# Transposing normalised rows through DRAM blocks and VectorE in place of TensorE and ScalarE

## The chip, the cores and the metric

The kernel runs on one core of a Trainium2 chip. The metric is the device time of one execution in microseconds, as the median of three runs. The engines are named as in the profile: PE is TensorE's matmuls, PEld its weight loads, DVE is VectorE, ACT is ScalarE, POOL is GpSimd, and SP is SyncE, whose only work here is to issue all DMAs, in one queue, in program order.

## What is computed

Two layers on a batch of 16 graphs of 1024 nodes with 256 channels, all in float32.

```python
# layer 0: aggregate over the normalised adjacency, two-layer perceptron with batch norms
x = _layernorm(x + _L0_gnn_ref(x, adj, W1, ..., be2))
# layer 1
c_adj = mean of x over channels                       # (B, N)
A     = |  |sigmoid(c_adj_j - c_adj_i) - 0.5| - 0.5 | * 2     # made symmetric
g     = relu(einsum('bcn,bnm->bcm', x^T, adj * A) * para)      # queries, channels first
k, v  = split(x @ kv_w)                                # 4 heads of 64
out   = softmax(q k^T * scale) v
x     = _layernorm(x + out)
```

The change concerns the x that enters layer 1, called x1 below. It is needed twice: with nodes on partitions (for the graph product and the last residual), and with channels on partitions, as x1T, because keys and values contract over channels.

## The kernel before

**Two stages.** Stage one, until about 820 us, is layer 0 up to the second batch norm's moments; its result y lies in DRAM. Stage two, `fast()`, takes the batches one by one: it finishes layer 0 for a batch, prepares layer 1 and runs attention. A general path, lines 1084 to 1193, is there for unusual softmax denominators and isn't entered.

**Steps and slots.** Attention of one batch is 16 steps (`step`, line 727). A step is `scores` (16 matmuls of 64x64 on 512 columns, line 739), `exps` (two exponentials on ScalarE, line 751), `sums` (VectorE adds them up for the denominators, lines 757 and 760) and `attend` (16 matmuls, line 770). All other work is cut into pieces and put into slots by `put(w, t, ...)`: batch w has slots 0 to 7. The loop from line 1055 emits the pieces of two slots, then four steps: slots 0 and 1, four steps, slots 2 and 3, four steps, and so on. This emission order is the order of each engine's queue; nothing reorders it later.

**The pieces that matter here.** In the slots of batch b-2 (lines 896 to 905), for each pair j = 0..3 of row blocks of batch b (one pair is 256 nodes):
- `load(b, j)`, slot j: four DMAs of 64 KB bring y in 32x32 blocks (`y_blk`, line 432), one DMA brings the old x (line 436)
- `bn2_q`, slot j+1: GpSimd applies batch norm 2 (line 599)
- `rows`, slot j+2: VectorE transposes the blocks (line 603), so that nodes lie on partitions, and adds x (line 604)
- `ln1_a`, slot j+2, and `ln1_b`, slot j+3: layer norm on VectorE (lines 547, 548, 624), with 1/sqrt on GpSimd (lines 66, 68); line 624 also gives the row sums
- `x1_t`, slot j+4: four TensorE transposes of 128x128 into PSUM (line 638) and a copy into x1T (line 639), by ScalarE for all batches but the first
- `means`, slot 6, and `crow`, slot 7: the row means (lines 642 and 644) are transposed (line 659), copied (line 661), and written to DRAM and read back on all partitions (lines 662 and 663)

In the slots of batch b-1: `wg_a` and `wg_b` (gates, slots 0 to 3, lines 671 to 680), `keys` (slots 0 and 1, line 688), `values` (slots 1 and 2, line 699), `graph` (32 products of 128x512, six or seven in each of slots 3 to 7, line 713) with `queries` after each eighth one (lines 721 and 722). In a batch's own slots, `dens`, `recips`, `finish_a`, `finish_s` and `finish_b` end each half of its nodes; `finish_b` issues the store of the result (line 841).

For batch 1 the slots of batch b-2 are slots -8 to -1. They are emitted before any attention, interleaved with the graph product of batch 0 (`opening`, line 1044), whose `queries` come in slot -1, and followed by `scores(0)`. Batch 0 itself has code of its own (lines 1018 to 1042) and keeps its TensorE transposes.

**Order inside a slot.** `arrange` (line 944) spreads pieces that are "short" on TensorE among the long ones and puts all others behind the last piece of lower or equal rank in `order` (line 930). `behind` (line 1058) marks the last short piece; `sums` of the next step is emitted there.

**Buffers.** The tag `yt` has two buffers (LDP = 2), x1T one per batch in flight (a pool of one), PSUM tag `t` four, exponentials six.

Of the kernel before, what the change touches and what calls it, by code (L numbers as in the profile page):

```python
# [9 lines left out]
F32 = mybir.dt.float32  # L10
# [6 lines left out]
P = 128  # L17
# [5 lines left out]
def gnn_norm_attention_kernel(  # L23
# [16 lines left out]
    nc = tc.nc  # L40
    B, N, C = x.shape
    H = W1.shape[0]
    NT = N // P
    CT = C // P
    HT = H // P
    FB = 512
    NH = N // FB
# [4 lines left out]
    dram = ctx.enter_context(tc.tile_pool(name="dram", bufs=1, space=DRAM))  # L52
# [28 lines left out]
    Q = 32  # L81
    NQ = P // Q
    y_blk = [yT_all[b].rearrange("i (d e) (q n) -> q e (i d) n", e=Q, q=NQ) for b in range(B)]
    st2_dram = dram.tile([2, C], F32, name="st2_d")

    c_dram = [dram.tile([NT, P], F32, name=f"crow_d{b}") for b in range(B)]
# [33 lines left out]
    with ExitStack() as l0:  # L120
# [32 lines left out]
        with ExitStack() as ph1:  # L153
# [9 lines left out]
            for i in range(0, NT, 2):  # L163
                t = hp.tile([P, 2, N], F32, tag="h", name=f"A{i}")
# [29 lines left out]
            for h in range(NH):  # L194
                rows = range(h * KB, (h + 1) * KB)
                for i in rows:
                    blk = A[i][:, ts(i, P)]
# [8 lines left out]
                for j in range(NT):  # L206
                    p = ps.tile([P, FB], F32, tag="ah"[j % 2], name="pat")
# [25 lines left out]
            for c in range(HT):  # L233
                p = ps.tile([P, FB], F32, tag="a", name="pw1")
# [3 lines left out]
            for c in range(CT):  # L238
                p = ps.tile([P, FB], F32, tag="a", name="pw2")
# [120 lines left out]
            def hidden(b, h, f):  # L360
                p = ps.tile([P, FB], F32, tag="h", name="ph")
                for k in range(CT):
                    nc.tensor.matmul(
                        p,
                        W1T[:, k, ts(f, P)],
                        aggT[b][:, k, ts(h, FB)],
                        start=(k == 0),
                        stop=(k == CT - 1),
                    )
                return p  # L370
# [11 lines left out]
            for f in range(HT):  # L382
                for h in range(NH):
# [3 lines left out]
                    p = hidden(B - 1, h, f)  # L387
# [7 lines left out]
        ldp = right("ldp", LDP)  # L395
# [43 lines left out]
        with ExitStack() as ph2:  # L439
# [74 lines left out]
            for k, pair in enumerate(pairs):  # L514
# [4 lines left out]
                if not ahead:  # L519
                    for j in range(LDP):  # L520
                        load(0, j)
                    for j in range(LDP, NT // 2):
                        t = accp.tile([P, 2, FB], F32, tag="acc", name=f"first{j}")
# [32 lines left out]
    def fast():  # L556
      with ExitStack() as fx:
# [15 lines left out]
        x1s, x1Ts, css, crows, mvs, wgs = {}, {}, {}, {}, {}, {}  # L573
# [46 lines left out]
        def ln1_b(b, j):  # L620
            mv, rs = mvs.pop((b, j))
            for a in range(2):
# [8 lines left out]
                    accum_out=css[b][:, 2 * j + a : 2 * j + a + 1],  # L631
                )

        def x1_t(b, j):
            p = ps_t.tile([P, CT, 2 * P], F32, tag="t", name="px")
            for a in range(2):
                for c in range(CT):
                    nc.tensor.transpose(p[:, c, ts(a, P)], x1s[b, j][:, a, ts(c, P)], ident)  # L638
            (nc.vector.tensor_copy if b == 0 else nc.scalar.copy)(x1Ts[b][:, :, ts(j, 2 * P)], p)  # L639

        def means(b):
            nc.vector.tensor_scalar_mul(css[b], css[b], 1.0 / C)
# [233 lines left out]
        def put(w, t, f, *a):  # L876
            at.setdefault(w * NC + t, []).append((f, a))
# [4 lines left out]
        for b in range(B):  # L882

            for hf in range(NH):
                t = (hf + 1) * (NC // NH)
                put(b, t, dens, b, hf)
                put(b, t + 1, recips, b, hf)
                for k in range(KB // 2):
                    put(b, t + 1 + k, finish_a, b, hf * (KB // 2) + k)
                    put(b, t + 1 + k, finish_s, b, hf * (KB // 2) + k)  # L890
                    late = NC - t - 2 - k if b == B - 1 and hf == 0 else 0
                    put(b, t + 2 + k + late, finish_b, b, hf * (KB // 2) + k)
            if b == 0:
                continue

            put(b - 2, 2, begin, b)
            for j in range(NT // 2):
                put(b - 2, j, load, b, j)
                put(b - 2, j + 1, bn2_q, b, j)
                put(b - 2, j + 2, rows, b, j)  # L900
                put(b - 2, j + 2, ln1_a, b, j)
                put(b - 2, j + 3, ln1_b, b, j)
                put(b - 2, j + 4, x1_t, b, j)
            put(b - 2, NC - 2, means, b)
            put(b - 2, NC - 1, crow, b)

            i = 0
            for t, n in enumerate(WG):
                for i in range(i, i + n):
                    put(b - 1, t, wg_a, b, i)  # L910
                    put(b - 1, t, wg_b, b, i)
                i += 1
            kv = [(keys, (b, c, h)) for c in range(CT) for h in range(NH)]
            kv += [(values, (b, j)) for j in range(0, NT, 2)]
            for t, n in enumerate(KV):
                for _ in range(n):
                    f, a = kv.pop(0)
                    put(b - 1, t, f, *a)
            m = 0
            for t, n in enumerate(QG):  # L920
                for m in range(m, m + n):
                    put(b - 1, NC - len(QG) + t, graph, b, m)
                m += 1
# [3 lines left out]
        nsteps = B * NS  # L927


        order = (dens, recips, finish_a, finish_b, x1_t, rows, ln1_a, ln1_b, finish_s, means, load, crow)  # L930
        rank = {f: k for k, f in enumerate(order)}
        short = (dens, recips, finish_a, x1_t, crow)
        long = (keys, values, graph)

        def spread(few, many):
# [119 lines left out]
        for t in range(min(at) // 2, max(max(at) // 2, nsteps // NK - 1) + 1):  # L1055
# [3 lines left out]
            for k in range(len(now) + 1):  # L1059
                if k == behind and 0 <= g < nsteps:  # L1060
                    sums(g)
                if k < len(now):
                    f, a = now[k]
# [15 lines left out]
        )  # L1079

    flag = fast()


# [153 lines left out]
```

## Time and profile before

| | before |
|---|---|
| time, median of 3 (range) | 2548.84 us (2546.09 to 2551.68) |
| span of the profiled execution | 2546.3 us |
| mean granted TensorE clock | 0.993 |
| PE, DVE, ACT, POOL busy | 98%, 68%, 42%, 34% |
| DMA: bytes, packets, of these under 512 B | 163.79 MB, 233,349, 136,680 |

Times in the profile are microseconds from the span's start. In a group of instructions the columns are line, engine and operation, tile written and tiles read with their shapes, count, then total busy time and the mean of one in nanoseconds, then the idle time of the engine just ahead of them and what ended it. In a timeline the columns are start, duration, engine, line, operation, tiles, count of merged neighbours, and in brackets the idle time before with its releaser. A matmul's duration is not its price where matmuls overlap; there the distance from one start to the next is the better measure. A long float32 product is issued as several instructions, so counts in the profile are multiples of the source's.

### The profile page before, as it was taken

How to read it: one execution, taken by the hardware profiler on the slowest of the kernel's cores; microseconds unless marked ns; L12 is line 12 of the kernel's file. 1: busy time of each engine (PE TensorE's matmuls, PEld its weight loads, DVE VectorE, ACT ScalarE, POOL GpSimd, SP SyncE). 2: the span in 40 equal slices, each digit the busy share in tenths (PEclk: the TensorE clock that was granted, in tenths of full speed). 3: DMA queues.
4: the chain of work that ended last, by engine and by line, in shares of the span. 5: the costliest groups of instructions: out<-in, count | busy, mean ns of one | idle time of the engine just before them, and what ended most of it. 6: DMA issues, size and time to landing. Idle time of an engine off the chain costs nothing. (4 is left out here: it accounts for less than half of the span.)

```text
span 2546.3 us, 33280 instructions
## 1 busy us (share of the span) xinstructions
PE 2487.9 (98%) x12813; PEld 1067.4 (42%) x12813; DVE 1730.6 (68%) x2594; ACT 1078.3 (42%) x1385; POOL 865.3 (34%) x766
## 2 busy tenths in 40 slices
PE   8999999998998999999999999999999999999997
PEld 4444444443443444344443444434444344443432
DVE  5545554556776776786877768777687776877556
ACT  2000000004453455465554655546556465564644
POOL 2222322222555323342433324333243332432132
PEclk9999999999999999999999999999999999999998
DMA  3122222230885201111111111111111111110000
GB/s 132 66 89 93 99 74 91 83 141 21 301 297 173 59 18 46 43 29 34 26 46 46 26 34 26 46 46 26 34 26 46 47 25 34 27 48 27 9 13 23
DMA packets 233349, 163.79 MB, mean 64 GB/s; under 512 B 136680, under 2 KB 221280, under 8 KB 226016
## 3 DMA queue, kind: packets, MB, share of 16 engines
q1 hardware_dynamic: 233184, 161.60, 21.1%
q8 instruction: 103, 1.69, 0.3%
q14 instruction: 62, 0.51, 0.1%
HBM read 98.58 MB, written 62.98 MB: 63 GB/s over the span
## 5 line engine op out<-in xcount | busy, mean ns | idle before, releaser
L751 ACT ACTIVATE e<-s 128x1024 f32<-128x1024 f32 x512 | 495.8, 1020 | 361.9 <-PE s L739 311.5
L760 DVE TENSOR_TENSOR acc<-acc,e 128x1024 f32<-128x1024 f32 x384 | 515.8, 1343 | 72.7 <-ACT e L751 42.6
L739 PE MATMUL s<-qT,kT 64*64 64x512 f32 x4096 | 492.4, 596 | 13.9 <-ACT e L751 13.2
L770 PE MATMUL o<-e,v 64*64 64x512 f32 x4096 | 486.4, 590 | 0.0
L713 PE MATMUL pg<-wg,x 128*128 128x512 f32 x960 | 434.5, 594 | 0.0
L822 POOL TENSOR_TENSOR r<-r,x 128x512 f32<-128x512 f32 x60 | 105.7, 1761 | 572.3 <-ACT wg L671 261.1
L739 PEld LDWEIGHTS s<-qT,kT 64*64 64x64 f32 x4096 | 147.2, 133 | 309.6 <-issue 250.9
L770 PEld LDWEIGHTS o<-e,v 64*64 64x64 f32 x4096 | 157.0, 133 | 284.1 <-issue 271.4
L599 POOL TENSOR_TENSOR yt<-yt,stq 128x512 f32<-128x512 f32 x120 | 192.4, 1603 | 193.2 <-DMA yt<-yT 188.3
L713 PEld LDWEIGHTS pg<-wg,x 128*128 128x128 f32 x960 | 172.3, 190 | 175.9 <-issue 166.1
L98 ACT COPY u<-pa 128x512 f32<-128x512 f32 x15 | 8.8, 585 | 475.3 <-PE pa L303 475.3
L680 DVE SCALAR_TENSOR_TENSOR wg<-wg,adj_sb 128x1024 f32<-128x1024 f32 x128 | 156.3, 1239 | 67.3 <-ACT wg L676 65.0
L303 PE MATMUL pa<-AhT,x 128*128 128x512 f32 x360 | 161.8, 592 | 0.0
L688 PE MATMUL pk<-x1T,kvw 128*128 128x512 f32 x256 | 118.4, 606 | 1.3 <-DVE x1T L639 1.3
L639 ACT COPY x1T<-px 128x512 f32<-128x512 f32 x60 | 35.1, 586 | 191.4 <-PE px L638 190.6
L699 PE MATMUL pv<-kvw,x1T 128*128 128x256 f32 x512 | 115.7, 379 | 0.0
L721 DVE TENSOR_TENSOR qT<-pg,para_sb 128x512 f32<-128x512 f32 x64 | 44.2, 690 | 101.7 <-PE pg L713 100.8
L334 PE MATMUL ph<-agg,SW 128*128 128x512 f32 x240 | 112.8, 592 | 0.0
L66 POOL TENSOR_SCALAR rs_a<-mv_a 128x2 f32<-128x2 f32 x64 | 20.5, 320 | 258.3 <-DVE mv_a L548 258.3
L303 PE MATMUL pa<-T,sx 128*128 128x512 f32 x240 | 107.9, 592 | 0.0
L303 PEld LDWEIGHTS pa<-AhT,x 128*128 128x128 f32 x360 | 68.4, 190 | 86.1 <-issue 86.1
L782 DVE TENSOR_TENSOR ot<-o,ot 128x512 f32<-128x512 f32 x64 | 44.0, 688 | 87.8 <-ACT ot L781 87.8
(193 smaller groups left out, 3332.4 us busy)
## 6 DMA issues: line engine op xcount, KB each, us to landing
h<-hT SPq DMA_DIRECT2D x28, 1024.0 KB, 4.4
hL<-h SPq DMA_DIRECT2D x28, 1024.0 KB, 9.2
x<-in_x_dram SPq DMA_DIRECT2D x16, 1024.0 KB, 7.3
yT<-y SPq DMA_DIRECT2D x64, 256.0 KB, 2.5
out_dram<-r SPq DMA_DIRECT2D x64, 256.0 KB, 2.1
xr<-in_x_dram SPq DMA_DIRECT2D x62, 256.0 KB, 2.9
yt<-yT SPq DMA_DIRECT2D x240, 64.0 KB, 2.9
crow<-crow_d SPq DMA_DIRECT2D x15, 512.0 KB, 4.0
```

The costliest lines, as they stand in the source:

```text
L303: nc.tensor.matmul(p, xs[n][:, k, :], bs[n][:, k, :], start=(k == 0), stop=(k == KN - 1))
L334: nc.tensor.matmul(p, ws[n][:, ts(f, P)], bs[n], start=True, stop=True)
L599: nc.gpsimd.tensor_tensor(y, y, sc, op)
L680: nc.vector.scalar_tensor_tensor(t, t, 1.0, adj_sb[:, i, :], op0=OP.add, op1=OP.mult)
L688: nc.tensor.matmul(p, kvw[:, k, ts(c, P)], x1Ts[b][:, k, ts(h, FB)], start=(k == 0), stop=(k == CT - 1))
L699: nc.tensor.matmul(p[:, ts(a, C)], x1Ts[b][:, k, ts(j + a, P)], kvw[:, k, C:], start=(k == 0), stop=(k == CT - 1),)
L713: nc.tensor.matmul(pg[b], x1s[b, k // 2][:, k % 2, ts(c, P)], wgs[b, k][:, ts(h, FB)], start=(k == 0), stop=(k == NT - 1))
L739: nc.tensor.matmul(t[r * HD : (r + 1) * HD, h, :], kTs[b, pair][h * HD : (h + 1) * HD, ts(2 * cb + r, HD)], qTs[b, pair, hf][h * HD : (h + ...
L751: nc.scalar.activation(E[g, a], S.pop((g, a)), AF.Exp)
L760: nc.vector.tensor_add(ACC[b, hf, pair], ACC[b, hf, pair], E[g, a])
L770: nc.tensor.matmul(O[b, hf, pair][r][h * HD : (h + 1) * HD, :], vs[b][r * HD : (r + 1) * HD, cb, pair * P + h * HD : pair * P + (h + 1) * HD],
L822: (nc.gpsimd if b < B - 1 else nc.vector).tensor_add(r, r, x1s.pop((b, j)))
```

## The change

For batches 1 to 15, x1T is no longer made by TensorE and ScalarE. `put_x1` writes the normalised rows to DRAM in two channel halves. `get_x1` reads them back with four DMAs of 64 KB, one for each group of 32 partitions, so that every 32x32 block lies in its final place but not yet transposed. `x1_v` transposes the blocks with one VectorE instruction of 128x512 straight into x1T. The buffer in between, XB, shares the tag `yt` and its two buffers with `load`. `put_x1` comes in slot j+3, `get_x1` in slot j+4, and `x1_v` in slot j+5, one slot later than `x1_t` was. The last x1_v of a batch (j = 3) so falls into slot 0 of batch b-1, where keys begin; therefore keys are now made by halves of nodes: both channel halves of nodes 0 to 511 in slot 0, those of nodes 512 to 1023 in slot 1. `x1_v` is not "short" any more, as it has no TensorE work. The aim is to take the transposes off TensorE's queue and the copies off ScalarE's.

```diff
+    x1_dram = {
+        (b, j): dram.tile([CT, 2 * P, P], F32, name=f"x1_{b}_{j}") for b in range(1, B) for j in range(NT // 2)
+    }
...
+        def put_x1(b, j):
+            for c in range(CT):
+                nc.sync.dma_start(
+                    x1_dram[b, j][c].rearrange("(a p) f -> p a f", p=P), x1s[b, j][:, :, ts(c, P)]
+                )
+
+        def get_x1(b, j):
+            t = XB[b, j] = ldp.tile([P, CT * 2 * P], F32, tag="yt", name=f"xb{b}_{j}")
+            blk = x1_dram[b, j].rearrange("c (m n) (q f) -> q n (c m) f", n=Q, q=NQ)
+            for q in range(NQ):
+                nc.sync.dma_start(
+                    t[q * Q : (q + 1) * Q].rearrange("p (m f) -> p m f", f=Q), blk[q]
+                )
+
+        def x1_v(b, j):
+            nc.vector.transpose(x1Ts[b][:, :, ts(j, 2 * P)], XB.pop((b, j)).rearrange("p (c n) -> p c n", c=CT))
...
-            (nc.vector.tensor_copy if b == 0 else nc.scalar.copy)(x1Ts[b][:, :, ts(j, 2 * P)], p)
+            nc.vector.tensor_copy(x1Ts[b][:, :, ts(j, 2 * P)], p)
...
-                put(b - 2, j + 4, x1_t, b, j)
+                put(b - 2, j + 3, put_x1, b, j)
+                put(b - 2, j + 4, get_x1, b, j)
+                put(b - 2, j + 5, x1_v, b, j)
...
-            kv = [(keys, (b, c, h)) for c in range(CT) for h in range(NH)]
+            kv = [(keys, (b, c, h)) for h in range(NH) for c in range(CT)]
...
-        order = (dens, recips, finish_a, finish_b, x1_t, rows, ln1_a, ln1_b, finish_s, means, load, crow)
+        order = (dens, recips, finish_a, finish_b, x1_v, rows, ln1_a, ln1_b, put_x1, get_x1, finish_s, means, load, crow)
         rank = {f: k for k, f in enumerate(order)}
-        short = (dens, recips, finish_a, x1_t, crow)
+        short = (dens, recips, finish_a, crow)
```

More of the change, by code (lines that the diff above doesn't have):

```diff
@@ L632, in ln1_b @@
                 )
+        XB = {}
+        def put_x1(b, j):
[12 more added lines that the diff above has]
+            nc.vector.transpose(x1Ts[b][:, :, ts(j, 2 * P)], XB.pop((b, j)).rearrange("p (c n) -> p c n", c=CT))
         def x1_t(b, j):
```

## The prediction

> **What bounds the kernel now.** I read the page's busy times first, then the groups of instructions, then the timeline of one batch in the middle of stage two, engine by engine, and last the stretch in which batch 1 is prepared.
>
> ```profile
> PE 2487.9 (98%) x12813; PEld 1067.4 (42%) x12813; DVE 1730.6 (68%) x2594; ACT 1078.3 (42%) x1385; POOL 865.3 (34%) x766
> ```
>
> TensorE is busy nearly always; work taken from its queue shortens the time, unless its gaps grow. The groups of the work concerned:
>
> ```profile
> L603 DVE STREAM_TRANSPOSE x<-yt 128x512 f32<-128x512 f32 x60 | 42.1, 702 | 0.0
> L638 PE MATMUL px<-ident,x 128*128 128x128 f32 x256 | 40.7, 282 | 2.3 <-ACT x L991 2.0
> L639 ACT COPY x1T<-px 128x512 f32<-128x512 f32 x60 | 35.1, 586 | 191.4 <-PE px L638 190.6
> ```
>
> The count at L638 has 16 transposes of batch 0, which stay. The new VectorE transpose has the very shape of L603. Next, TensorE's timeline in slots 4 to 7 of one batch:
>
> ```profile
> 1455.91 2.11 PE L791 MATMUL pd<-acc,ones 128*32 128x512 f32 x8
> 1457.95 0.66 PE L638 MATMUL px<-ident,x 128*128 128x128 f32 x4
> 1458.44 5.32 PE L713 MATMUL pg<-wg,x 128*128 128x512 f32 x12
> ...
> 1484.05 0.66 PE L813 MATMUL pf<-ident,ot 128*128 128x128 f32 x4
> 1484.55 3.60 PE L713 MATMUL pg<-wg,x 128*128 128x512 f32 x8
> 1487.98 0.60 PE L638 MATMUL px<-ident,x 128*128 128x128 f32 x4
> 1488.42 2.74 PE L713 MATMUL pg<-wg,x 128*128 128x512 f32 x6
> 1490.99 0.60 PE L638 MATMUL px<-ident,x 128*128 128x128 f32 x4
> 1491.43 3.60 PE L713 MATMUL pg<-wg,x 128*128 128x512 f32 x8
> 1494.87 0.27 PE L659 MATMUL pc<-ident,cs 128*8 128x128 f32 x1
> ```
>
> From start to next start four transposes cost 0.44 us (1487.98 to 1488.42, and twice more), 0.49 us behind L791. The L791 of this slot 4 takes 2.11 us; that of slot 0 takes 1.06 (1511.54): in slots 0 to 3 VectorE's sums are late by 1 us and TensorE waits, in slots 4 to 7 nothing stops it. VectorE in the same slots:
>
> ```profile
> 1470.69 0.70 DVE L603 STREAM_TRANSPOSE x<-yt 128x512 f32<-128x512 f32 x1
> 1475.11 7.87 DVE L760 TENSOR_TENSOR acc<-acc,e 128x1024 f32<-128x1024 f32 x6
> 1484.77 0.69 DVE L782 TENSOR_TENSOR ot<-o,ot 128x512 f32<-128x512 f32 x1 [1.80 <-ACT ot L781]
> 1489.04 0.17 DVE L644 TENSOR_SCALAR hcs<-cs 128x8 f32<-128x8 f32 x1
> 1497.76 0.69 DVE L721 TENSOR_TENSOR qT<-pg,para_sb 128x512 f32<-128x512 f32 x1 [5.13 <-PE pg L713]
> ```
>
> It has 1.80 us free at 1483 and 5.13 us ahead of 1497.76.
>
> **What the skill says.** "TensorE: Matmul & The Clock Gate", Part 4, has about 275 ns for a transpose inside a kernel. The trace's records are 272 to 273 ns, but the starts are 0.11 us apart; priced by the record 240 transposes would be 65 us, by the starts 26. The starts decide. "VectorE: DVE Perf Modes", The three transpose paths, says that VectorE transposes 32x32 blocks only; hence the detour by DRAM. "DMA: Bandwidth & Descriptors", Anatomy of one DMA, has a fixed cost of about 2 us, mostly the receipt of the last byte (it measures another issue path). Here the 64 KB block loads land 1.9 to 4.3 us after their issue begins, median 2.9: agreement, and a chain cost that bandwidth doesn't hide.
>
> **The change part by part.**
>
> *Removed, TensorE:* four quartets a batch, 0.49 + 3 x 0.44 = 1.81 us. Batches 2 to 15 have them inside attention: 14 x 1.81 = 25.3 us, all on the path. *Removed, ScalarE:* 60 x 0.586 = 35.1 us; ScalarE waits for TensorE ahead of these copies, so I give nothing for it.
>
> *Added, VectorE:* 60 x 0.702 = 42.1 us, four a batch. j = 3 falls into slot 0, at 1407.2 of the batch shown, where VectorE idles 2.47 us ahead of 1409.64 for a gate: free, although the late half of slots 0 to 3 is VectorE's. j = 0 is in slot 5, ahead of the 1.80 us gap; j = 1 and 2 in slots 6 and 7, ahead of the 5.13 us gap. Hidden.
>
> *Added, SyncE:* six DMAs a pair. An issue takes about 0.45 us and four block loads 2.0, so 2.9 us a pair and 11.5 a batch of 105.8: room enough. After its last issue a load is there 2.0 us later (1445.88 to 1447.83), at worst 3.4 (1499.1 to 1502.52). So from the end of line 624 to usable XB: put of the next pair 0.9 + get 2.0 + landing 2.0 to 3.4 = 4.9 to 6.3 us; I take 5.0 where little else moves.
>
> *Waits in attention.* x1_v(0): get(0) is issued after put(1), which needs line 624 of pair 1, done at 1460.85; XB is there at 1465.8 to 1467.2. In VectorE's queue come first recips, queries, finish_a and the sum of line 757, which depend on TensorE and end near 1470. No wait. x1_v(1): get(1) follows line 624 of pair 2 (1474.1), there by 1480.4, wanted at 1486. No wait. x1_v(2): line 624 of pair 3 ends near 1487.5, XB is there at 1492.4 to 1493.8; VectorE reaches it near 1490 and waits 2.4 to 4 us. Behind it are the sum of line 757 and the queries of 1497.76, for which it waits anyway until TensorE is through (1495.9 after the change): hidden. x1_v(3): loaded by 1497, wanted at 1405.4 + 105.8 or later. Keys by halves read pairs 0 and 1 first, pairs 2 and 3 in slot 1: no wait.
>
> *A moved piece, crow.* Without x1_t it is the first TensorE piece of slot 7, with seven products between finish_a and it: 0.44 + 7 x 0.86 = 6.46 us after L813 begins; before it was 10.8. It needs the means, whose first half (L642) ends 4.96 us after L813 begins in each batch shown by the timeline. Slack 1.50, less the 0.70 of x1_v(1) between them: 0.80 us. Free, but the narrowest margin.
>
> *Moved loads.* load(3) now stands behind put(0) in SyncE's queue and comes some 3 us later, load(1) of the next batch waits for x1_v(3); both are wanted 4 us or more later by VectorE. Free.
>
> *Batch 1, in the opening.* Here slots -4 to -1 have no attention steps between them, so put, get and x1_v follow each other at once and VectorE's queue stands:
>
> ```profile
> 874.82 0.27 PE L659 MATMUL pc<-ident,cs 128*8 128x128 f32 x1
> 875.02 1.09 PE L739 MATMUL s<-qT,kT 64*64 64x512 f32 x8
> ...
> 893.05 2.00 PE L739 MATMUL s<-qT,kT 64*64 64x512 f32 x16 [2.78 <-ACT e L751]
> ```
>
> Line 624 of pair 1 ends at 866.7. XB(0) 5.0 later, x1_v(0) done at 872.4. The same VectorE work as before (866.67 to 870.08) puts line 624 of pair 2 at 875.9; x1_v(1) 5.7 later, 881.6; line 624 of pair 3 at 882.5, means 882.8, then batch 0's queries, which ended near 877 before and now near 887. TensorE's scores(0) stand behind these. SyncE: put(3) 883.4, get(2) 885.4, get(3) 887.4, and only then crow's store, before at 875.78: 11.6 us later. The gates start 5.3 us behind that store (881.10), ScalarE runs gates up to exponentials and TensorE's 893.05 waits for these. So everything is 11.6 us late, once. Bounds: 8 if the landings overlap better, 15 with 3.4 us landings in both places.
>
> *Sum:* 2548.84 - 25.3 + 11.6 = 2535.1 us.
>
> **Rivals.**
> - *The opening costs nothing:* queries or crow slip in earlier than I read the order, and 2548.84 - 25.3 = 2523.5. Against it: the order puts get_x1(3) ahead of crow and queries behind x1_v(1). Chance 0.13.
> - *x1_v(3) lands in VectorE's late half:* with slots 0 to 3 VectorE's, 14 x 0.70 = 9.8 us come back: 2544.9, no change that can be told. For it: L791's 2.11. Against it: the 2.47 us gap. Chance 0.10.
> - *TensorE waits in each batch:* if XB comes late enough that crow, the sums or a PSUM buffer hold TensorE by 2.7 us a batch (0.80 of slack gone, landings at 6 us), 14 x 2.7 = 37.8 is lost: 2535.1 + 37.8 = 2572.9, slower. Against it: landings of at most 4.3. At 1.8 us a batch only the opening would remain, 2560.4. Chance 0.13 for this family.
> - The forecast itself, 0.64.
>
> **How the numbers follow.** The forecast with its bounds on the opening is 2531 to 2539, the first rival 2523.5, the second 2544.9. The range from 2522 to 2553 takes in these and the mild end of the third. Faster by over 0.2% (under 2543.7): 0.64 + 0.13 = 0.77. Within: 0.10. Slower: 0.13.
>
> **What would show it.** L638 with 16 left; a VectorE transpose into x1T of about 0.70 us x60; slots 4 to 7 of a batch 1.8 us shorter, a batch of about 104.0 instead of 105.8; no wait of L659 for VectorE's cs inside attention; VectorE standing some 5 us ahead of x1_v(0) and x1_v(1) of batch 1 and 2.4 to 4 us ahead of x1_v(2) in the others; the first scores near 885 instead of 875. I am wrong if L791 of slot 0 grows over 1.06 us, if L791 of slot 4 grows over 2.11, or if the opening doesn't grow.

## The result

| | before | after |
|---|---|---|
| time, median (range) | 2547.47 us (2546.06 to 2551.68) | 2537.45 us (2535.91 to 2540.48) |
| ratio, 95% interval | | 0.9959 (0.9942 to 0.9977) |
| span of the profiled execution | 2546.3 us | 2538.7 us |
| attention, one batch (median in the trace) | 105.80 us | 104.10 us |

The changed kernel is 10.0 us faster, 0.41% with an interval of 0.23 to 0.58%. The prediction was 2535.1 us, from 2522 to 2553. The kernel before was run a fourth time, so its median here is 2547.47 us and not the 2548.84 us from which the prediction started.

The page of the changed kernel, busy times:

```profile
PE 2471.2 (97%) x12573; PEld 1048.0 (41%) x12573; DVE 1765.1 (70%) x2654; ACT 1042.9 (41%) x1325; POOL 876.9 (35%) x766
```

TensorE has 240 matmuls fewer and ScalarE 60 instructions fewer, VectorE has 60 more. The answer on the tile x1T shows the new transpose and what is left of the old way, which is batch 0's:

```profile
L656 DVE STREAM_TRANSPOSE x1T<-xb x60: 699/703/712, 874.6 to 2352.4; 128x512 f32<-128x512 f32 x60
L663 DVE COPY x1T<-px x4: 658/680/682, 828.0 to 834.3; 128x512 f32<-128x512 f32 x4
```

TensorE's timeline in slots 4 to 7, one batch in the middle, as shown of before:

```profile
1464.33 2.12 PE L815 MATMUL pd<-acc,ones 128*32 128x512 f32 x8
1466.37 5.42 PE L737 MATMUL pg<-wg,x 128*128 128x512 f32 x12
...
1491.64 0.66 PE L837 MATMUL pf<-ident,ot 128*128 128x128 f32 x4
1492.14 6.17 PE L737 MATMUL pg<-wg,x 128*128 128x512 f32 x14
1498.15 0.27 PE L683 MATMUL pc<-ident,cs 128*8 128x128 f32 x1
1498.26 6.17 PE L737 MATMUL pg<-wg,x 128*128 128x512 f32 x14
...
1518.26 1.07 PE L815 MATMUL pd<-acc,ones 128*32 128x512 f32 x8
```

The px transposes are gone, and nothing stands in their place: products follow each other, pc (crow, L683) has no wait. From L815 of slot 4 to L815 of the next slot 0 it is 53.93 us; before it was 55.63 (1455.91 to 1511.54). L815 of slot 4 still takes 2.12 us and that of slot 0 takes 1.07 (2.11 and 1.06 before), so VectorE's lateness in slots 0 to 3 is as it was. VectorE in the same slots:

```profile
1478.50 0.70 DVE L656 STREAM_TRANSPOSE x1T<-xb 128x512 f32<-128x512 f32 x1
1479.76 0.71 DVE L606 STREAM_TRANSPOSE x<-yt 128x512 f32<-128x512 f32 x1 [0.55 <-POOL r L846]
1484.19 7.87 DVE L784 TENSOR_TENSOR acc<-acc,e 128x1024 f32<-128x1024 f32 x6
1492.37 0.69 DVE L806 TENSOR_TENSOR ot<-o,ot 128x512 f32<-128x512 f32 x1 [0.31 <-ACT ot L805]
1493.57 0.70 DVE L656 STREAM_TRANSPOSE x1T<-xb 128x512 f32<-128x512 f32 x1
1496.71 0.14 DVE L666 TENSOR_SCALAR cs<-cs 128x8 f32<-128x8 f32 x1
1496.88 0.17 DVE L668 TENSOR_SCALAR hcs<-cs 128x8 f32<-128x8 f32 x1
1501.46 0.71 DVE L656 STREAM_TRANSPOSE x1T<-xb 128x512 f32<-128x512 f32 x1 [2.82 <-DMA xb<-x]
1504.47 0.69 DVE L745 TENSOR_TENSOR qT<-pg,para_sb 128x512 f32<-128x512 f32 x1 [1.19 <-PE pg L737]
1519.59 0.70 DVE L656 STREAM_TRANSPOSE x1T<-xb 128x512 f32<-128x512 f32 x1
```

The four block transposes are L656. The third one waits 2.82 us for its data, and the queries (L745) behind it still wait 1.19 us for TensorE: the DMA wait is hidden. The 1.80 us of before ahead of ot have shrunk to 0.31. Then the opening, VectorE's timeline first:

```profile
874.62 0.71 DVE L656 STREAM_TRANSPOSE x1T<-xb 128x512 f32<-128x512 f32 x1 [5.75 <-DMA xb<-x]
...
883.79 0.71 DVE L656 STREAM_TRANSPOSE x1T<-xb 128x512 f32<-128x512 f32 x1 [5.15 <-DMA xb<-x]
```

and TensorE's:

```profile
819.37 2.38 PE L618 MATMUL py<-ident,yt 128*128 128x128 f32 x8 [5.38 <-ACT yt L584]
...
885.63 0.37 PE L683 MATMUL pc<-ident,cs 128*8 128x128 f32 x1 [9.82 <-DVE cs L666]
887.40 3.97 PE L763 MATMUL s<-qT,kT 64*64 64x512 f32 x16 [1.40 <-DVE qT L745]
...
908.46 3.48 PE L763 MATMUL s<-qT,kT 64*64 64x512 f32 x16 [3.13 <-ACT e L775]
```

and SyncE's, with crow's store:

```profile
886.31 4.19 SPq L651 DMA_DIRECT2D xb<-x  x8
890.60 0.38 SPq L686 DMA_DIRECT2D crow_d<-crow  x1
```

Before, stage two and crow's store began so:

```profile
815.56 2.38 PE L615 MATMUL py<-ident,yt 128*128 128x128 f32 x8 [5.38 <-ACT yt L581]
...
875.78 0.34 SPq L662 DMA_DIRECT2D crow_d<-crow  x1
```

VectorE stands 5.75 and 5.15 us, TensorE waits 9.82 us for the means behind it, crow's store stands behind eight block loads in SyncE's queue, and the scores that began at 893.05 before begin at 908.46. Of these 15.4 us, 3.8 are not the change's: stage one, which it leaves alone, ended later in this execution (the first transposes of stage two at 819.37 instead of 815.56; in the executions below at 814.4 to 816.4). So up to these scores the opening is about 11.6 us longer. To the first L815 it is 13.1 us longer (125.50 us from the first transposes of stage two, 112.43 before); the 1.5 us in between fall where TensorE's granted clock drops, which the part on the prediction takes up.

VectorE's first wait doesn't count from the rows that it needs: pair 0 was put from 865.56 on, but in SyncE's queue `get_x1` of pair 0 (870.29) stands behind `put_x1` of pair 1 (869.26), which waits for the rows of pair 1. Whether another order of these two would shorten the opening was not tried.

### The profile page after: what moved, and what is told of

It is laid out like the page before. It is cut to its first block, busy times and chain, and to the rows that moved or that the text cites. A ratio compares the mean times of both kernels' runs of the same rounds, so it can differ in the third digit from the quotient of the medians.

```text
span 2538.7 us, 33394 instructions
## 1 busy us (share of the span) xinstructions
PE 2471.2 (97%) x12573; PEld 1048.0 (41%) x12573; DVE 1765.1 (70%) x2654; ACT 1042.9 (41%) x1325; POOL 876.9 (35%) x766
## 5 line engine op out<-in xcount | busy, mean ns | idle before, releaser
L784 DVE TENSOR_TENSOR acc<-acc,e 128x1024 f32<-128x1024 f32 x384 | 522.2, 1360 | 73.1 <-ACT e L775 41.7
L737 PE MATMUL pg<-wg,x 128*128 128x512 f32 x960 | 429.0, 595 | 0.0
L846 POOL TENSOR_TENSOR r<-r,x 128x512 f32<-128x512 f32 x60 | 115.7, 1928 | 555.5 <-DVE r L841 352.2
L862 ACT ACTIVATE r<-r,nm,rs_z 128x256 f32<-128x256 f32 x128 | 69.8, 594 | 121.2 <-POOL nm L854 121.2
L745 DVE TENSOR_TENSOR qT<-pg,para_sb 128x512 f32<-128x512 f32 x64 | 44.2, 690 | 86.9 <-PE pg L737 86.9
L723 PEld LDWEIGHTS pv<-kvw,x1T 128*128 128x128 f32 x512 | 94.9, 190 | 14.6 <-ACT kT L715 1.6
L482 PE MATMUL po<-hL,SV 128*128 128x512 f32 x224 | 98.4, 592 | 0.0
```

The lines of the kernel that those rows point to most:

```text
L723: nc.tensor.matmul(p[:, ts(a, C)], x1Ts[b][:, k, ts(j + a, P)], kvw[:, k, C:], start=(k == 0), stop=(k == CT - 1),)
L737: nc.tensor.matmul(pg[b], x1s[b, k // 2][:, k % 2, ts(c, P)], wgs[b, k][:, ts(h, FB)], start=(k == 0), stop=(k == NT - 1))
L784: nc.vector.tensor_add(ACC[b, hf, pair], ACC[b, hf, pair], E[g, a])
L846: (nc.gpsimd if b < B - 1 else nc.vector).tensor_add(r, r, x1s.pop((b, j)))
```

## The experiments

The theory: TensorE's queue is shorter by 14 x 1.70 = 23.8 us, VectorE's and SyncE's additions lie in gaps, and the opening gives back 12 to 14 us once. The rivals: the shortfall is spread over the batches or comes from more DMA traffic; ScalarE's copies were part of the gain; SyncE's queue, not VectorE's, makes the opening longer; VectorE is near its limit. In the table, differences are to the median of the kernel before in the same series (2547.47 us for the changed kernel, 2549.02 for the next four, 2547.07 for the last four). A ratio is to the kernel before. Distances between batches are medians in the trace.

| kernel | median us | difference us | ratio (95% interval) |
|---|---|---|---|
| changed kernel | 2537.45 | -10.0 | 0.9959 (0.9942 to 0.9977) |
| batch 1 the old way | 2525.63 | -23.4 | 0.9904 (0.9889 to 0.9919) |
| only batch 1 the new way | 2560.95 | +11.9 | 1.0048 (1.0034 to 1.0061) |
| batch 1: crow ahead of two loads | 2532.22 | -16.8 | 0.9936 (0.9922 to 0.9950) |
| TensorE transposes put back, unread | 2561.37 | +12.4 | 1.0047 (1.0032 to 1.0063) |
| ScalarE copies put back, unread | 2537.28 | -9.8 | 0.9956 (0.9940 to 0.9973) |
| block transposes twice | 2537.85 | -9.2 | 0.9956 (0.9939 to 0.9972) |
| block transposes four times | 2559.40 | +12.3 | 1.0040 (1.0026 to 1.0055) |
| keys in the old order | 2537.82 | -9.3 | 0.9961 (0.9947 to 0.9976) |

**Batch 1 the old way.** Batch 1 goes back to TensorE transposes and ScalarE copies; batches 2 to 15 keep the new way.

```diff
-            nc.vector.tensor_copy(x1Ts[b][:, :, ts(j, 2 * P)], p)
+            (nc.vector.tensor_copy if b == 0 else nc.scalar.copy)(x1Ts[b][:, :, ts(j, 2 * P)], p)
...
+                if b == 1:
+                    put(b - 2, j + 4, x1_t, b, j)
+                    continue
                 put(b - 2, j + 3, put_x1, b, j)
...
-        short = (dens, recips, finish_a, crow)
+        short = (dens, recips, finish_a, x1_t, crow)
```

> Batch 1 goes back to TensorE transposes and ScalarE copies in slots -4 to -1; batches 2 to 15 keep the new way. Theory (the opening loses 12 to 14 us, once, because put, get and block transpose follow each other with nothing between; the rest of the change is worth 14 x 1.70 = 23.8 us): 2547.5 - 23.8 = 2523.7 us, batches still 104.10 us apart, the first scores of attention at 875 to 878 in the trace. Rival (the shortfall against 25.3 us is spread over the batches, or comes from the added DMA traffic or a lower granted clock): 2532 to 2537 us.

Measured 2525.63 us, 23.4 under the kernel before, with batches 104.10 us apart. TensorE's timeline, next to 875.02 and 893.05 of before:

```profile
875.15 1.09 PE L763 MATMUL s<-qT,kT 64*64 64x512 f32 x8
...
893.77 2.78 PE L763 MATMUL s<-qT,kT 64*64 64x512 f32 x16 [3.13 <-ACT e L775]
```

The opening up to these scores is as before (77.42 us from the first transposes of stage two, 77.49 before), and the whole of 14 x 1.70 = 23.8 us stays. DMA traffic can't be the cause of the shortfall: this kernel moves 56 of the 60 pairs through DRAM. It is faster than both kernels, and all it takes is to leave batch 1 out of the change.

**Only batch 1 the new way.** The same edit with `b > 1` in place of `b == 1`.

> Only batch 1 goes the new way; batches 2 to 15 go back to TensorE transposes and ScalarE copies (keys stay by halves of nodes). Theory: 2547.5 + 12 to 14 = 2559.5 to 2561.5 us, batches 105.80 us apart. Rival (the opening is nearly free): 2546 to 2550 us.

Measured +11.9 us, batches 105.81 us apart. The two halves of the change, run apart, give -23.4 and +11.9, together -11.5; the change itself measured -10.0. The difference is within what the medians scatter.

**Crow ahead of two loads, batch 1 only.** `get_late` is `get_x1` under a name that has no rank, so that it comes behind crow.

```diff
+                late = b == 1 and j >= 2
+                put(b - 2, NC - 1 if late else j + 4, get_late if late else get_x1, b, j)
+                put(b - 2, NC if late else j + 5, x1_v, b, j)
```

> As the changed kernel, but for batch 1 the loads get_x1 of pairs 2 and 3 are issued behind crow's store and read, and their block transposes come in slot 0. Theory (most of the opening's loss is VectorE standing ahead of the first two block transposes, 10 to 11 us, and SyncE's queue ahead of crow adds about 4): crow's store 4.1 us earlier, 2537.5 - 4 = 2533.5 us. Rival 1 (SyncE's queue ahead of crow is the loss): 2524 to 2527 us. Rival 2 (VectorE's waits are all of it, crow's place is worth nothing): 2537.5 us.

Measured 6.8 us less than the changed kernel by the differences to before. In the traces, from the first transposes of stage two to the first L815 it is 121.33 us, against 125.50 in the changed kernel: 4.2 us. SyncE's and TensorE's timelines of it:

```profile
880.59 0.89 SPq L643 DMA_DIRECT2D x<-x  x2
881.66 0.34 SPq L689 DMA_DIRECT2D crow_d<-crow  x1
883.05 0.35 SPq L690 DMA_DIRECT2D crow<-crow_d  x1
883.56 4.67 SPq L651 DMA_DIRECT2D xb<-x  x8
```

```profile
880.92 0.37 PE L686 MATMUL pc<-ident,cs 128*8 128x128 f32 x1 [9.69 <-DVE cs L669]
...
891.68 3.67 PE L715 MATMUL pk<-x1T,kvw 128*128 128x512 f32 x8 [1.44 <-DVE x1T L659]
...
900.80 2.00 PE L766 MATMUL s<-qT,kT 64*64 64x512 f32 x16
```

Crow's store now precedes the eight block loads and comes 4.0 us earlier, as the theory said (67.25 us after the first transposes of stage two, against 71.23 in the changed kernel), while the wait of 9.69 us behind VectorE remains. The scores that began at 908.46 in the changed kernel come only 2.7 us earlier (86.39 us after the first transposes, against 89.09): keys now wait 1.44 us for the block transposes that were moved. The other 1.5 of the 4.2 us are the drop of the granted clock, which this trace doesn't have. The 6.8 us of the medians hold about 2.6 more, which the opening doesn't show; the ranges of the two kernels (2530.62 to 2535.16, 2535.91 to 2540.48) allow for it. Rival 1, which had SyncE's queue as the whole loss, asked for some 12 us and falls; rival 2, which had crow's place as nothing, falls too.

**TensorE transposes put back, unread.** Beside the new way, in the old slot, for batches 2 to 15; their result is not used.

```diff
+        def ghost(b, j):
+            p = ps_t.tile([P, CT, 2 * P], F32, tag="t", name="pghost")
+            for a in range(2):
+                for c in range(CT):
+                    nc.tensor.transpose(p[:, c, ts(a, P)], x1s[b, j][:, a, ts(c, P)], ident)
...
+                if b > 1:
+                    put(b - 2, j + 4, ghost, b, j)
...
-        short = (dens, recips, finish_a, crow)
+        short = (dens, recips, finish_a, ghost, crow)
```

> As the changed kernel, with the four TensorE transposes of each pair of batches 2 to 15 done again in slot j+4, into PSUM, read by nobody. Theory (the gain is TensorE's queue alone): the whole gain comes back as loss, 2537.5 + 14 x 1.70 = 2561.3 us, batches 105.80 us apart. Rival (half or more of the gain is ScalarE's copies or their hold on PSUM): 2549 us or less.

Measured 2561.37 us, batches 105.81 us apart as before the change. 22.4 us came back (12.4 + 10.0): the gain is TensorE's queue.

**ScalarE copies put back, unread.** As the last one, but `ghost` holds `nc.scalar.copy(p, x1s[b, j])`, of the same size as the old copy, though from SBUF into PSUM and not the other way; its result is not used.

> As the changed kernel, with a ScalarE copy of 128x512 (x1 into PSUM, read by nobody) for each pair of batches 2 to 15 in slot j+4, where the copy into x1T was: ScalarE's part of the removed work put back alone. Theory (ScalarE's 35.1 us were worth nothing): 2537.5 us, within 2. Rival (ScalarE's copies were part of the gain): 2545 us or more.

Measured 2537.28 us. The 56 copies put back are 32.8 us of ScalarE's work and cost nothing that can be measured.

**Block transposes twice, and four times.** For batches 2 to 15; the repeats write the same values. The fourfold kernel has 4 in place of 2.

```diff
+            for _ in range(2 if b > 1 else 1):
+                nc.vector.transpose(x1Ts[b][:, :, ts(j, 2 * P)], xb)
```

> As the changed kernel, but each block transpose into x1T of batches 2 to 15 is done twice, 56 x 0.70 = 39.3 us more on VectorE. Theory (block transposes lie in VectorE's gaps; the narrowest margin, crow's, is 1.3 us in the trace): 2537.5 us, within 2, batches 104.10 us apart. Rival (VectorE sets the pace in part of a batch): 14 x 0.70 to 56 x 0.70 more, 2547 to 2577 us.

> As the changed kernel, but each block transpose of batches 2 to 15 is done four times, 118 us more on VectorE. Theory (the gaps are 0.3 us ahead of the end of slot 5, 1.3 us ahead of crow and 1.9 us in slot 0, so 1.8 us of slot 5's and 2.1 us of slot 6's added work less 1.3 hold TensorE at crow): about 2.6 us a batch, 2537.5 + 36 = 2574 us, with L683 waiting for VectorE's cs in every batch. Rival A (all of it counts): 2655 us. Rival B (gaps are wider than read): 2537.5 us.

Twice: 2537.85 us; 39 us more of block transposes cost nothing that can be measured. Not all of it went into gaps: VectorE's busy time grew by 27.8 us only (1765.1 to 1792.9), as line 627 takes 52.4 us in all instead of 61.6; the reason is below. Four times: 2559.40 us, 21.9 more than the changed kernel, where the theory had 36: the place was right, the size was not. TensorE's and VectorE's timelines of the fourfold kernel:

```profile
1496.73 0.65 PE L839 MATMUL pf<-ident,ot 128*128 128x128 f32 x4
1497.22 6.17 PE L739 MATMUL pg<-wg,x 128*128 128x512 f32 x14
1504.83 0.27 PE L685 MATMUL pc<-ident,cs 128*8 128x128 f32 x1 [1.43 <-DVE cs L668]
```

```profile
1498.62 0.68 DVE L808 TENSOR_TENSOR ot<-o,ot 128x512 f32<-128x512 f32 x1
1499.82 2.94 DVE L658 STREAM_TRANSPOSE x1T<-xb 128x512 f32<-128x512 f32 x4
1502.69 0.44 DVE L627 SCALAR_TENSOR_TENSOR x<-x,mv_a,rs_a 128x256 f32<-128x256 f32 x1
1504.54 0.14 DVE L668 TENSOR_SCALAR cs<-cs 128x8 f32<-128x8 f32 x1
```

TensorE waits 1.43 us at crow, where the theory had 2.6. From pf to ot it is now 1.89 us, 1.16 more than the 0.73 of the changed kernel and not 1.8, since the wait of 0.55 us for GpSimd ahead of L606 is gone; and the two instructions of line 627 need 0.92 us there instead of 1.56, as GpSimd's residual add no longer lies beside the first (1.09 us in the changed kernel, 0.44 here). 1.16 + 2.24 - 0.64 - 1.30 = 1.46 us, close to the 1.43. In all a batch is 105.68 us long, 1.58 more, and all of it lies in slots 4 to 7: from pf to crow's pc it is 8.10 us instead of 6.51, so the stop costs 1.6 us, a little more than the wait of 1.43 that the profile shows. Slots 0 to 3 take what they took (50.16 us). 14 x 1.58 = 22.1 us, what was measured.

**Keys in the old order.**

```diff
-            kv = [(keys, (b, c, h)) for h in range(NH) for c in range(CT)]
+            kv = [(keys, (b, c, h)) for c in range(CT) for h in range(NH)]
```

> As the changed kernel, with keys in the old order (both halves of nodes of channel half 0 first). Theory: the last block transpose is done about 2 us into slot 0 and before the second key begins, so TensorE doesn't wait: 2537.5 us, within 2. Rival (keys wait for the last pair in every batch): 1 to 2 us a batch, 2551 to 2565 us.

Measured 2537.82 us. The last block transpose is done at 1520.29 in the changed kernel's trace, 2 us into slot 0 and ahead of the second key. The new order of keys isn't needed for the time.

## Why the prediction was right

- *Removed, TensorE, 25.3 us:* 23.8 in the trace (14 x 1.70), 23.4 and 22.4 by the two kernels that isolate it. The price by starts was right; the record's 0.27 us for a transpose would have given 65. The 0.11 us a batch too many are the quartet behind L791, which I priced at 0.49 us: the products that now follow L815 take 5.42 us for what took 5.32, so a part of those 0.49 us stays with whatever comes after the small matmuls.
- *Removed, ScalarE, nothing:* shown by the copies put back.
- *Added, VectorE, hidden:* shown by doubling, with the help of line 627. The wait of the third block transpose was given as 2.4 to 4 us and is 2.82. The first, second and fourth don't wait, as said. The slack at crow, given as 0.80 us, is 1.3: from the end of cs (1496.84) to L683 (1498.15). I had set the whole 0.70 us against it, but in the changed kernel cs ends 5.20 us after pf begins, only 0.24 later than before. Part of what the block transpose adds is made up again, mainly by the two instructions of line 627, which take 1.56 us here and took 1.96 before (line 624 there), as they now come later in GpSimd's residual add beside them. The prediction took the work between as fixed and had no term for this.
- *Moved loads, free:* slots 0 to 3 take 50.17 us, before 50.15.
- *Opening, 11.6 us:* +11.9 us when only batch 1 is changed. In the trace the two waits of VectorE are 5.75 and 5.15 us where 5.0 each was expected, and crow's store comes 11.0 us later against the first transposes of stage two (60.22 before, 71.23 after), where 11.6 was expected. Its split is shown too: with crow ahead of the loads the store came 4.0 us earlier.
- *Sum:* the predicted gain was 13.7 us (25.3 - 11.6), the measured one is 10.0. Of the 3.7 us between them, 1.5 are the transposes, and about 1.5 are TensorE's clock (from the scores at 908.46 to the first L815 it is 36.41 us, before 34.94), for which the prediction had no term; what is left is no more than the medians scatter. That the predicted time lies only 2.4 us under the median is luck in part: the 2548.84 us it started from were 1.4 above the median of four runs. The clock: in the trace of the changed kernel the granted clock is 0.72 for some 6 us from 908 on, and was 1.00 there before. It was 0.68 at the same place in the kernel with batch 1 the old way, so it doesn't need the longer opening. In the traces here it goes with how long TensorE stopped just ahead of these scores: it drops in all eight kernels in which that was 2.97 to 3.13 us, and not before (2.78 us) nor with crow ahead of two loads (no such stop). That the stop is the cause was not tried.

Of the rivals, the free opening falls by the second kernel. The block transpose in VectorE's late half falls by slots 0 to 3, and the wait of TensorE in each batch by L683, which has none inside attention.

## What to carry to other kernels

The detour by DRAM cost 5 to 6 us of latency a piece here (store issue, load issue, landing; 5.75 and 5.15 us where nothing covered it): it was free where the queue that waits for it has other work between the load and the use, and fully paid where the pipeline is being filled and that work is missing. So treat the first item of a pipelined loop apart: here the change on all batches but the first one in the pipeline is worth 23 us, on all of them 10. And price a pipelined matmul by the distance of starts, and test a hidden addition by doubling it, but look in the trace at what else got shorter: here a neighbour did.

## What I had not expected of the hardware

- The same VectorE instruction of line 627, with two SBUF inputs (rows of 128x256 and a column spread to that size), took 0.44 us with GpSimd idle and 1.09 us beside GpSimd's add, so that adding 2.2 us of transposes ahead of it made it 0.65 us shorter. The Trainium skill, "SBUF — State Buffer", Who interferes with whom, says that a VectorE instruction with two SBUF inputs contends with a GpSimd instruction that reads SBUF, and that the port pair they share is an exclusive lock. The traces agree: the instruction that began beside the add ended 0.28 us after the add's end (1495.01), and 0.28 us after it in the kernel before as well (1487.58).
- Four float32 transposes of 128x128 between other matmuls cost TensorE 0.44 us by starts but 0.27 us each by their records.
- In the changed kernel TensorE's granted clock fell to 0.50 towards the end of its wait of 9.82 us (1.00 from 876 to 880, 0.50 from 882 to 890), so that the 16 matmuls of scores behind it took 3.97 us instead of the 1.95 of those at 901.18. This cost nothing here, as ScalarE then waited for crow until 896.50. In the kernel before, without such a wait, it was 1.00 from 862 to 890.
